# Four selective-scan layers on one NeuronCore: in the middle layers, one of the four input products of a scan group is made by TensorE

## The chip, the cores and the metric

The kernel runs on one NeuronCore of a Trainium2 chip, all in float32. The metric is the device time of one execution in microseconds. Six engines matter: PE (TensorE, with its weight loads apart as PEld), DVE (VectorE), ACT (ScalarE), POOL (GpSimd), SP (SyncE, which issues the DMAs) and the DMA engines themselves. SBUF is the memory that all of them read; PSUM takes what PE writes, in eight banks of 512 float32 per partition.

## The reference

The input is an image batch x of 4 x 48 x 48 x 192. Four layers follow each other, and all are built around the same selective scan. For channels d and 16 states n it is, in the words of the reference's second middle layer:

```python
def step(h_prev, t):
    x_t, dt_t, B_t, C_t = t
    dA = jnp.exp(dt_t[..., None] * A)
    dBx = (dt_t * x_t)[..., None] * B_t[:, :, None, :]
    h = dA * h_prev + dBx
    y = jnp.einsum('bkdn,bkn->bkd', h, C_t)
    return (h, y)
```

- Layer 0 is a bidirectional Mamba over the columns, a norm, and another over the rows: 16 passes over an image's 2304 tokens.
- Layers 1 and 2, the middle layers, are scans in four directions (rows, columns, both reversed) for each of four images: `dts, Bs, Cs` come from one projection of the input, `delta = softplus(dts @ W + bias)`, and the four results are summed. A norm, in layer 1 also a gate and a projection, closes each.
- Layer 3 runs short Mamba scans along each row and each column, and an MLP ends the network.

## The kernel before

**Tiling.** A pass over an image is cut into six jobs of 384 tokens (`CH`); a job's last states enter the next. In the middle layers the 192 channels are cut into three blocks of 64, and the 128 partitions hold a block twice: the upper half works on states 0 to 7, the lower on 8 to 15 (`parts` = 2). The eight states of each half make two groups of four (`NG`). A job so has 3 blocks x 2 groups = 6 steps, which I number as slots 0 to 5; the odd ones have group 1. Two layers, four images, four passes and six jobs make 192 jobs, 1152 steps. In layer 0 and in the rows (`parts` = 1) a block has 128 channels, a job four groups and 12 steps.

**One step**, for block i and group g:

- `decay` (L437), ACT: four `a = exp(delta * A)`, one per state. In the iteration before a new block, `enter` (L470) stands between the third and the fourth: the copy of `du` (delta times x) into a PSUM bank.
- `scan` (L475), DVE: the product `inputs = du * B` for all four states, 128 x 1540 (each state has 384 tokens and one entry column for the carried state), and one scan over the 1540 into `h`. `gather` puts its waits on an instruction ahead of it.
- `weigh` (L501), POOL: the last column of h is kept as the carried `state`, then h is multiplied by C in place. `carry` (L455) has written the states of the job before into B's entry column.
- `reduce` (L516), PE: four matmuls add the four states into `y` in PSUM, a half of the partitions each. With group 0, `skip` (L561) opens y: it adds the result of an earlier pass (`prior`) and, in the last pass of an image, the skip term D * x.

After the second group of a block, `take` copies y to `yc` (ACT), `gate` adds its two halves by a matmul into a `ps` buffer, and `close` (L577) copies that into a tile `o` (ACT), which is stored after the third block.

**The job ahead.** While a job runs, the next one's inputs are made (`units` L557, `projections` L383): in slot 1 the x_proj matmuls into a `ps` buffer and their copy `bcd`, which `spread` (L412) sends to memory as rows of B and C; in slot 2 the three `delta` (a matmul and an ACT softplus each). The softplus and the exp need different tables, so two table loads fall into each job. `fetch` (L422) brings B and C of one group back, each row spread over 64 partitions, two DMAs per group. `drive` (L465, POOL) multiplies delta by x for a block, into `dus`. Norm steps of the images before (`Side`) run in some slots on PE, ACT and POOL.

**What sets the order.** `run_jobs` (L1029) writes the order of every queue out by hand. Everything on ACT, POOL, DVE and PE runs in program order on its engine: L59 and L104 are the helpers through which the instructions pass, so most of them bear one of these two lines in the profile. In the middle layers, iteration t issues: scan(t), decay(t+2) with the fetch and the enter in it, close and take of an earlier block, carry(t+1), weigh(t), the next job's units, side work, gate (even t), drive (odd t), reduce(t-1). PSUM has one bank for y (L269), two rotating `ps` buffers (L270) for everything that PE makes on the side, four banks for `inputs` and one for `du`.

**What layer 0 and the rows have already.** There the class `MambaJob` overrides four of these functions. Two of the four products of a step are made by PE (`MADE` = 2): `turn` (L685) transposes du through a `ps` buffer, and ACT copies it to `duT`; `fill` (L710) multiplies duT by diagonal matrices with B's values on the diagonal, so that the product lands in a PSUM tile `made`. The diagonals come from memory: `spread` (L641) writes B's values, one element at a time, along the diagonals of zeroed buffers `dg`, and `fetch` (L662) brings them with the rows. DVE then multiplies only two states (`given`), and scans `made` by itself. There reduce runs two iterations behind the scan, not one.

The functions that the change touches, and what calls them:

Of the kernel before, what the change touches and what calls it, by code (L numbers as in the profile page):

```python
# [28 lines left out]
MADE = 2  # L29
LINE = 3 * MADE * 128  # L30

# [30 lines left out]
class K:  # L62
# [100 lines left out]
    def mean_weights(self, n):  # L163
        w = self.tile(self.const, [Q, Q], f"mean{n}")
        self.nc.vector.memset(w, 1.0 / n)
        return w
# [82 lines left out]
class ScanPools:  # L249
# [6 lines left out]
    def __init__(self, k, ctx, parts, rows):  # L256
# [6 lines left out]
        self.made = parts == 1  # L263
# [9 lines left out]
        self.given = NG - MADE if self.made else NG  # L273
# [7 lines left out]
        if self.made:  # L281
            self.made_inputs = k.tile(self.vec, [128, 1024], "made")[:, 512 - CH : 512 + CH]
            self.n_jobs = 0
            self.diags = []
            zeros = self.decays[2].rearrange("p j l -> p (j l)")[:, : LINE + 1]
            k.g.memset(zeros, 0.0)
            for n in range(2 * self.groups):
                d = k.dram([128 * (LINE + 1)], "dg")
                k.nc.sync.dma_start(d.rearrange("(t x) -> t x", x=LINE + 1), zeros)
                self.diags.append(d)  # L290
# [41 lines left out]
class ScanJob:  # L332
# [16 lines left out]
    def turn(self, i):  # L349
        pass  # L350

    def turn_back(self, i):
        pass

    def fill(self, i, g):
        pass
# [55 lines left out]
    def spread(self):  # L412

        self.bc = self.k.dram([2 * N, self.pools.W], "bc")
        self.k.nc.sync.dma_start(self.bc, self.bcd[: 2 * N, :])
# [6 lines left out]
    def fetch(self, g):  # L422

        k, pools = self.k, self.pools
        wide = pools.wide
        both = k.tile(pools.bcs, [128, 2, NG, pools.W], "bcb")
        self.bcb[g] = both[:, 0, :, :], both[:, 1, :, self.tokens]
        self.fetched[g] = []
        for m in range(pools.parts):
            at = (m * pools.groups + g) * 2 * NG  # L430
            ins = k.nc.sync.dma_start(
                both[m * wide : (m + 1) * wide].rearrange("p s j l -> p (s j l)"),
                self.bc[at : at + 2 * NG, :].rearrange("r l -> (r l)").partition_broadcast(wide),
            )
            self.fetched[g].append(ins)

    def decay(self, i, g, between=None):  # L437

        k, w, pools = self.k, self.w, self.pools
        if i == 0:  # L440
            self.fetch(g)
# [32 lines left out]

    def scan(self, i, g):  # L475

        k, pools = self.k, self.pools
        b, du, W = pools.b, pools.du, pools.W
        waits = self.waits.pop((i, g))
        if g == 0:  # L480
            waits.append(pools.entered)
        if pools.n_h >= pools.hbufs:
            of = pools.n_h - pools.hbufs
            waits += [pools.readers[of], pools.weighed[of]]
        pools.n_h += 1
        k.gather(waits)
        k.v.tensor_tensor(
            b, du.unsqueeze(1).to_broadcast([128, NG, W]), self.bcb[g][0], ALU.mult
        )
        step = -1 if self.rev else 1  # L490
        h = self.h[i, g] = k.tile(pools.hs, [128, NG, W], "h")
        k.v.tensor_tensor_scan(
            h.rearrange("p j l -> p (j l)")[:, ::step],
            self.a.pop((i, g)).rearrange("p j l -> p (j l)")[:, ::step],
            b.rearrange("p j l -> p (j l)")[:, ::step],
            0.0,
            ALU.mult,
            ALU.add,
        )
# [36 lines left out]
class DirJob(ScanJob):  # L536
# [11 lines left out]
    def load(self):  # L548
        k, two = self.k, self.pools.two
        self.xs = k.tile(two, [128, 3, CH], "xs")  # L550
        for m in range(2):
            k.nc.sync.dma_start(self.xs[m * 64 : (m + 1) * 64], self.part(self.src))
        if self.prior is not None:
            self.added = k.tile(two, [64, 3, CH], "added")
# [22 lines left out]
    def close(self, i):  # L577
        if i == 0:
            self.o = self.k.tile(self.pools.two, [64, 3, CH], "o")
        self.k.copy(self.o[:, i, :], self.ys)  # L580
        if i == 2:
            self.k.nc.sync.dma_start(self.part(self.dst), self.o)
# [5 lines left out]
class MambaJob(ScanJob):  # L588
# [52 lines left out]
    def spread(self):  # L641

        k, pools = self.k, self.pools
        sync = k.nc.sync
        n = pools.groups * (pools.given + NG)
        self.bc = k.dram([n, pools.W], "bc")
        sync.dma_start(self.bc, self.bcd[:n, :])
        be = k.dram([pools.groups, MADE, CH], "be")
        sync.dma_start(be.rearrange("g e l -> (g e) l"), self.bcd[n : 2 * N, self.tokens])
        at = pools.n_jobs % 2 * pools.groups  # L650
        pools.n_jobs += 1
        self.lines = pools.diags[at : at + pools.groups]
        for g in range(pools.groups):
            line = self.lines[g].rearrange("(t x) -> t x", x=LINE + 1)[:, :LINE]
            line = line.rearrange("t (b e c) -> t b e c", b=3, c=128)
            for e in range(MADE):
                with k.nc.allow_non_contiguous_dma(reason="diagonal"):
                    sync.dma_start(
                        line[:, :, e, 0:1], be[g, e].rearrange("(b t v) -> t b v", t=128, v=1)
                    )  # L660

    def fetch(self, g):  # L662

        k, pools = self.k, self.pools
        rows = pools.given + NG
        n = rows * pools.W
        t = k.tile(pools.bcs, [128, n + LINE], "bcb")
        both = t[:, :n].rearrange("p (j l) -> p j l", l=pools.W)
        self.bcb[g] = (
            both[:, : pools.given, :],  # L670
            both[:, pools.given :, self.tokens],
            t[:, n:].rearrange("p (b e c) -> p b e c", b=3, c=128),
        )
        ins = k.nc.sync.dma_start(
            t[:, :n],
            self.bc[g * rows : (g + 1) * rows, :]
            .rearrange("r l -> (r l)")
            .partition_broadcast(128),
        )
        k.nc.sync.dma_start(  # L680
            t[:, n:], self.lines[g][: 128 * LINE].rearrange("(t x) -> t x", t=128)
        )
        self.fetched[g] = [ins]

    def turn(self, i):  # L685

        k, pools = self.k, self.pools
        ps = k.tile(pools.ps, [128, 512], "ps")[:, :CH]
        self.turned_over(ps, self.du[i])
        self.duT[i] = k.tile(pools.two, [128, CH], "duT")  # L690
        k.copy(self.duT[i], ps)
        self.xd = k.tile(pools.one, [128, CH], "xd")
        k.act(self.xd, self.xs[:, i, :], AF.Identity, scale=self.w.D[:, i, :])
# [15 lines left out]

    def fill(self, i, g):  # L710

        k, pools = self.k, self.pools
        for b in range(3):
            at = slice(b * 128, (b + 1) * 128)
            for e in range(MADE):
                k.t.matmul(
                    pools.made_inputs[:, e * CH : (e + 1) * CH][:, at],
                    self.duT[i][:, at],
                    self.bcb[g][2][:, b, e, :],
                    start=True,  # L720
                    stop=True,
                    skip_group_check=True,
                )

    def scan(self, i, g):

        k, pools = self.k, self.pools
        waits = self.waits.pop((i, g))
        if g == 0:
            waits.append(pools.entered)  # L730
        if pools.n_h >= pools.hbufs:
            of = pools.n_h - pools.hbufs
            waits += [pools.readers[of], pools.weighed[of]]
        pools.n_h += 1
        k.gather(waits)
        n = pools.given
        du = pools.du.unsqueeze(1).to_broadcast([128, n, pools.W])
        k.v.tensor_tensor(pools.b, du, self.bcb[g][0], ALU.mult)
        step = -1 if self.rev else 1
        h = self.h[i, g] = k.tile(pools.hs, [128, NG, pools.W], "h")  # L740
        a = self.a.pop((i, g))

        def scan(at, tokens, b, first=0.0):
            k.v.tensor_tensor_scan(
                *(v[:, at, tokens].rearrange("p j l -> p (j l)")[:, ::step] for v in (h, a)),
                b[:, ::step],
                first,
                ALU.mult,
                ALU.add,
            )  # L750

        scan(slice(0, n), slice(0, pools.W), pools.b.rearrange("p j l -> p (j l)"))
        if pools.rows:
            scan(slice(n, NG), self.tokens, pools.made_inputs)
            return
        for e in range(MADE):
            at = g * NG + n + e
            first = 0.0 if self.prev is None else self.prev.state[:, i, at : at + 1]
            scan(
                slice(n + e, n + e + 1),  # L760
                self.tokens,
                pools.made_inputs[:, e * CH : (e + 1) * CH],
# [1393 lines left out]
```

## Time and profile before

| | us |
|---|---|
| median of 3 runs (18010.82 to 18017.85) | 18016.21 |
| the profiled execution | 18024.41 |
| its span, from the first instruction to the last | 18022.6 |
| layer 0 | about 49 to 5700 |
| inputs of the middle layers (convolutions, norm) | about 5700 to 6080 |
| middle layers | about 6080 to 12145 |
| rows | about 12300 to 17600 |
| MLP | to the end |

Busy over the whole span, from the page: PE 16243.2 us (90%), DVE 16418.0 (91%), ACT 13776.3 (76%), POOL 14149.0 (79%). A share of the whole is a mean over stages that differ, so the stages are read one by one. A group line names source line, engine, operation, output and inputs by the program's names, then count, busy time and mean duration in ns, then how long the engine stood idle ahead of it and what ended that. In a timeline each line has start and duration in us, and in brackets the idle time before it. PE records two matmul passes for each float32 matmul, one for a transpose, and its durations contain the pipeline's drain, so starts are the better measure of its pace.

### The profile page before, as it was taken

The numbers are of one execution on the slowest core, as the hardware profiler recorded it, in microseconds if no ns is written. First come the engines' busy times: TensorE is split into PE (matmuls) and PEld (weight loads), VectorE is DVE, ScalarE is ACT, GpSimd is POOL, SyncE is SP. The second block draws the span as 40 slices with busy tenths as digits, with TensorE's granted clock in tenths as the row PEclk, the third lists the DMA queues.
The fourth block names the chain that finished last, engine by engine and source line by source line (L and its number), as shares of the span: only waits on it lengthen the run. The fifth ranks groups of instructions, "written<-read, shape, count | busy, mean of one in ns | idle before, by whom it ended". The sixth has DMA issues, their size and how long they took to land. (4 is left out here: it accounts for less than half of the span.)

```text
span 18022.6 us, 313028 instructions
## 1 busy us (share of the span) xinstructions
PE 16243.2 (90%) x118512; PEld 10759.8 (60%) x118512; DVE 16418.0 (91%) x10747; ACT 13776.3 (76%) x25601; POOL 14149.0 (79%) x10862
## 2 busy tenths in 40 slices
PE   9999999999999777787777877878999999999999
PEld 7787787888885322222222222226888888888874
DVE  8899899999996799999999999996999999999992
ACT  7888888888885567777777777777888888888874
POOL 7877878878874488888888888876888888888880
PEclk9999999999999878788888887789999999999999
DMA  4343343333333466666666666663343343433431
GB/s 137 122 128 124 125 134 122 128 126 128 128 126 93 105 137 146 151 148 153 152 148 149 144 150 140 147 145 112 122 127 125 120 124 123 132 123 122 125 118 50
DMA packets 1229187, 2324.58 MB, mean 129 GB/s; under 512 B 704376, under 2 KB 962016, under 8 KB 1075232
## 3 DMA queue, kind: packets, MB, share of 16 engines
q1 hardware_dynamic: 1227680, 2304.55, 46.8%
q8 instruction: 938, 15.37, 0.4%
q14 instruction: 569, 4.66, 0.1%
HBM read 2105.57 MB, written 200.98 MB: 128 GB/s over the span
## 5 line engine op out<-in xcount | busy, mean ns | idle before, releaser
L59 POOL TENSOR_TENSOR h<-h,bcb 128x1536 f32<-128x1536 f32 x3456 | 11312.2, 3273 | 798.6 <-DVE h L59 499.1
L104 ACT ACTIVATE a<-delta,A 128x384 f32<-128x384 f32 (+1 forms) x13824 | 7377.6, 603 | 911.7 <-DVE h L59 901.2
L59 DVE TENSOR_TENSOR_SCAN h<-a,inputs 128x770 f32<-128x770 f32 (+2 forms) x3456 | 7915.9, 2290 | 146.5 <-DVE inputs L59 1.8
L59 DVE TENSOR_TENSOR inputs<-du,bcb 128x770 f32<-128x770 f32 (+2 forms) x3456 | 4256.4, 1232 | 287.2 <-POOL bcb L59 100.9
L59 PE MATMUL made<-bcb,duT 128*128 128x128 f32 x27648 | 3559.6, 279 | 172.1 <-DVE h L59 139.6
L59 PEld LDWEIGHTS y<-ident,h 128*128 128x128 f32 x27648 | 3119.8, 142 | 845.0 <-issue 485.7
L59 PE MATMUL y<-ident,h 128*128 128x128 f32 x27648 | 3508.5, 277 | 59.8 <-ACT yt L104 49.2
L59 PEld LDWEIGHTS made<-bcb,duT 128*128 128x128 f32 x27648 | 3341.4, 195 | 273.9 <-DVE h L59 178.7
L59 PE MATMUL y<-h,sum 128*64 128x384 f32 x9216 | 2661.7, 643 | 750.2 <-POOL h L59 547.4
L59 DVE TENSOR_TENSOR_SCAN h<-a,made 128x768 f32<-128x768 f32 (+1 forms) x1536 | 2343.2, 1536 | 263.2 <-PE made L59 256.4
L59 PEld LDWEIGHTS y<-h,sum 128*64 128x64 f32 x9216 | 848.7, 167 | 2175.9 <-issue 982.2
L59 DVE TENSOR_TENSOR_SCAN h<-a,state,made 128x384 f32<-128x384 f32 x1920 | 1827.8, 993 | 221.1 <-PE made L59 219.4
L59 POOL COPY state<-h 128x4 f32<-128x4 f32 x2304 | 434.4, 189 | 1908.5 <-DVE h L59 1879.5
L59 PE MATMUL ps<-bcd,dtT 12*128 12x384 f32 (+1 forms) x2304 | 1076.9, 580 | 245.1 <-ACT delta L104 240.2
L59 PE MATMUL ps<-u,inT 96*128 96x384 f32 x3456 | 1251.7, 489 | 38.8 <-DMA u<-xn_wh 27.1
L104 ACT ACTIVATE delta<-ps,vec 128x384 f32<-128x384 f32 x1152 | 636.4, 577 | 344.3 <-PE ps L59 338.2
L59 PEld LDWEIGHTS ps<-bcd,dtT 12*128 12x128 f32 (+1 forms) x2304 | 415.1, 206 | 808.8 <-ACT delta L104 487.3
L59 PE MATMUL ps<-yt,outT 128*96 128x384 f32 x2304 | 808.7, 488 | 0.4 <-POOL yt L59 0.4
L59 PE MATMUL ps<-xh,diag 32*32 32x192 f32 x32256 | 796.8, 324 | 4.0 <-ACT xc L104 2.3
L59 PEld LDWEIGHTS ps<-u,inT 96*128 96x128 f32 x3456 | 600.5, 191 | 304.0 <-issue 36.4
L104 ACT ACT_TABLE_LOAD x603 | 773.6, 1283 | 10.6
L101 ACT ACT_TABLE_LOAD x600 | 769.8, 1283 | 9.8 <-PEq L2146 0.7
(147 smaller groups left out, 15082.7 us busy)
## 6 DMA issues: line engine op xcount, KB each, us to landing
bcb<-bc SPq DMA_DIRECT2D x768, 770.0 KB
bcb<-bc SPq DMA_DIRECT2D x384, 1155.0 KB
bcb<-bc SPq DMA_DIRECT2D x384, 1152.0 KB
bcb<-dg SPq DMA_DIRECT2D x768, 384.0 KB
y<-o SPq DMA_DIRECT2D x192, 288.0 KB
xs<-xi_wh SPq DMA_DIRECT2D x96, 288.0 KB
xs<-xi_hw SPq DMA_DIRECT2D x96, 288.0 KB
added<-y SPq DMA_DIRECT2D x96, 288.0 KB
```

Source lines behind the costliest of these rows:

```text
L59: return lambda *a, **kw: self.tc.keep_in_program_order(op(*a, **kw))
L101: self.in_order(self.nc.scalar.preload_act_table_set(LOG_EXP))
L104: return self.in_order(self.nc.scalar.activation(out, in_, func, **kw))
```

## The change

`MADE` becomes a table: two made products with `parts` = 1, one with `parts` = 2. The functions `spread`, `fetch`, `turn`, `fill` and `scan` of `MambaJob` move into the base class, written for both cases, so that the middle layers use them as well. A middle step then has three products on DVE (128 x 1155), a scan over these, and a scan of 384 over the made one, which starts from the carried state. `fill` makes the fourth product with two matmuls per 128 tokens, one for each half of the partitions. PSUM: three banks for `inputs`, one for `made`.

In `run_jobs` the fetch leaves `decay` and gets a place of its own after the scan, four groups ahead in the middle layers (two, as before, elsewhere). `turn` stands at the end of an even iteration, behind reduce and ahead of fill; `drive` goes from three groups ahead to four. `close` writes into the tile `added`, which held the prior's part, now with three buffers and taken in every pass; `o` goes. The weights of the 96-channel mean move from a lasting pool into that of their stage. On the host, the rows of the x_proj weights are put in the new order.

```diff
-MADE = 2
-LINE = 3 * MADE * 128
+MADE = {1: 2, 2: 1}
...
-        self.made = parts == 1
+        self.made = MADE[parts]
+        self.turned = parts == 1
+        self.line = 3 * self.made * parts * 128
...
-        self.given = NG - MADE if self.made else NG
+        self.given = NG - self.made
...
     def spread(self):
-        self.bc = self.k.dram([2 * N, self.pools.W], "bc")
-        self.k.nc.sync.dma_start(self.bc, self.bcd[: 2 * N, :])
+        k, pools = self.k, self.pools
+        sync, parts, made = k.nc.sync, pools.parts, pools.made
+        n = parts * pools.groups * (pools.given + NG)
+        self.bc = k.dram([n, pools.W], "bc")
+        sync.dma_start(self.bc, self.bcd[:n, :])
+        be = k.dram([parts, pools.groups, made, CH], "be")
+        sync.dma_start(be.rearrange("m g e l -> (m g e) l"), self.bcd[n : 2 * N, self.tokens])
...
+            for e in range(made):
+                for m in range(parts):
+                    with k.nc.allow_non_contiguous_dma(reason="diagonal"):
+                        sync.dma_start(
+                            line[:, :, e, m, 0:1],
+                            be[m, g, e].rearrange("(b t v) -> t b v", t=128, v=1),
+                        )
...
     def decay(self, i, g, between=None):
         k, w, pools = self.k, self.w, self.pools
-        if i == 0:
-            self.fetch(g)
...
+    def turn(self, i):
+        k, pools = self.k, self.pools
+        wide = pools.wide
+        ps = k.tile(pools.ps, [128, 512], "ps")[:, : 3 * wide]
+        for b in range(3):
+            k.t.matmul(
+                ps[:, b * wide : (b + 1) * wide],
+                self.du[i][:wide, b * 128 : (b + 1) * 128],
+                k.ident[:wide, :wide],
...
+        self.duT[i] = k.tile(pools.two, [128, 3, wide], "duT")
+        k.copy(self.duT[i].rearrange("p b d -> p (b d)"), ps)
+
+    def fill(self, i, g):
+        k, pools = self.k, self.pools
+        wide = pools.wide
+        for b in range(3):
+            for e in range(pools.made):
+                at = e * CH + b * 128
+                for m in range(pools.parts):
+                    k.t.matmul(
+                        pools.made_inputs[m * wide : (m + 1) * wide, at : at + 128],
+                        self.duT[i][:, b, :],
+                        self.bcb[g][2][:, b, e, m, :],
...
     def scan(self, i, g):
...
+        scan(slice(0, n), slice(0, pools.W), pools.b.rearrange("p j l -> p (j l)"))
...
+        for e in range(pools.made):
+            at = g * NG + n + e
+            first = 0.0 if self.prev is None else self.prev.state[:, i, at : at + 1]
+            scan(
+                slice(n + e, n + e + 1),
+                self.tokens,
+                pools.made_inputs[:, e * CH : (e + 1) * CH],
+                first,
+            )
...
     def close(self, i):
-        if i == 0:
-            self.o = self.k.tile(self.pools.two, [64, 3, CH], "o")
-        self.k.copy(self.o[:, i, :], self.ys)
+        self.k.copy(self.added[:, i, :], self.ys)
         if i == 2:
-            self.k.nc.sync.dma_start(self.part(self.dst), self.o)
+            self.k.nc.sync.dma_start(self.part(self.dst), self.added)
...
-    behind = 2 if jobs[0].pools.made else 1
-    ahead, taken, gated, driven = 2, behind + 1, behind + 2, 2 + behind
+    behind = 2 if jobs[0].pools.turned else 1
+    ahead, taken, gated, driven = 2, behind + 1, behind + 2, 4
+    fetched = 2 * ahead if behind == 1 else ahead
...
+        if t + fetched < len(groups) and groups[t + fetched][1] == 0:
+            job, i, g = groups[t + fetched]
+            job.fetch(g)
...
-        if soon := at_group(t + 2, 0):
+        if behind == 2 and (soon := at_group(t + 2, 0)):
             soon[0].turn(soon[1])
...
         if 0 <= t - behind < len(groups) and behind == 1:
             job, i, g = groups[t - behind]
             job.reduce(i, g)
+        if behind == 1 and (soon := at_group(t + 2, 0)):
+            soon[0].turn(soon[1])
         if t + 1 < len(groups):
             job, i, g = groups[t + 1]
             job.fill(i, g)
```

## The prediction, made before the change was run

> **What bounds the kernel now.** I read the windows by stage first, then the groups of instructions inside the middle stage and inside layer 0 (which already has what the change brings), then the timeline of one job. By stage (columns: busy time of PE, weight load, DVE, ACT, POOL, then granted clock, DMA share, GB/s):
>
> ```profile
> 6080.00:12145.00 6065.00, 4714.70 (x14810) 1607.45 (x14810) 5910.93 (x2304) 4404.79 (x8203) 5032.24 (x4284) 0.80 0.65 146
> 49.00:5700.00 5651.00, 5562.26 (x48933) 4497.28 (x48933) 5182.31 (x4641) 4651.70 (x8699) 4445.95 (x4197) 0.98 0.39 125
> 12300.00:17600.00 5300.00, 5084.91 (x51911) 4228.68 (x51909) 4982.67 (x3457) 4290.40 (x8000) 4607.83 (x2322) 0.99 0.40 124
> ```
>
> The first line is the stage that changes: DVE is busy 5911 of 6065 us (97%), and PE runs at a mean clock of 0.80. The other two stages keep their instructions. [...] The groups from 7000 to 11000 us:
>
> ```profile
> L59 POOL TENSOR_TENSOR h<-h,bcb 128x1536 f32<-128x1536 f32 x761 | 2621.2, 3444 | 61.5 <-POOL state L59 0.7
> L59 DVE TENSOR_TENSOR_SCAN h<-a,inputs 128x1540 f32<-128x1540 f32 x761 | 2557.7, 3361 | 29.3 <-DVE inputs L59 0.5
> L59 DVE TENSOR_TENSOR inputs<-du,bcb 128x1540 f32<-128x1540 f32 x761 | 1347.0, 1770 | 66.7 <-POOL bcb L59 22.6 <-PE y L59 10.0 <-ACT du L104 7.5
> ```
>
> 761 steps in 4000 us are 5.26 us each, 31.5 per job. DVE sets the pace and waits for almost nothing. The same groups in layer 0, 1000 to 5000 us:
>
> ```profile
> L59 POOL TENSOR_TENSOR h<-h,bcb 128x1536 f32<-128x1536 f32 x828 | 2410.8, 2912 | 66.8 <-POOL state L59 0.6
> L59 DVE TENSOR_TENSOR_SCAN h<-a,inputs 128x770 f32<-128x770 f32 x827 | 1453.0, 1757 | 30.1
> L59 DVE TENSOR_TENSOR_SCAN h<-a,state,made 128x384 f32<-128x384 f32 x1367 | 1301.4, 993 | 158.3 <-PE made L59 157.0
> L59 DVE TENSOR_TENSOR inputs<-du,bcb 128x770 f32<-128x770 f32 x828 | 797.1, 963 | 53.0 <-POOL bcb L59 52.3 <-DMA bcb<-bc 0.4
> ```
>
> Last, the timeline of one middle job, ACT from slot 1 to slot 3, with PE's x_proj matmuls and the DVE product that ends the stretch:
>
> ```profile
> 9016.65 2.14 PE L59 MATMUL ps<-xs,xpT 64*44 64x384 f32 x6
> 9018.13 0.47 ACT L104 ACTIVATE o<-ps 64x384 f32<-64x384 f32 x1
> 9018.87 0.48 ACT L104 ACTIVATE bcd<-ps 44x384 f32<-44x384 f32 x1
> 9020.51 2.13 ACT L104 ACTIVATE a<-delta,A 128x384 f32<-128x384 f32 x4 [1.16 <-DVE h L59]
> 9022.66 1.28 ACT L104 ACT_TABLE_LOAD   x1
> 9023.96 1.05 ACT L104 ACTIVATE delta<-ps,vec 128x384 f32<-128x384 f32 x2
> 9026.27 0.58 ACT L104 ACTIVATE delta<-ps,vec 128x384 f32<-128x384 f32 x1 [1.26 <-PE ps L59]
> 9026.87 1.28 ACT L101 ACT_TABLE_LOAD   x1
> 9028.17 1.63 ACT L104 ACTIVATE a<-delta,A 128x384 f32<-128x384 f32 x3
> 9029.70 0.47 ACT L104 ACTIVATE du<-dus 128x384 f32<-128x384 f32 x1
> ...
> 9030.91 1.77 DVE L59 TENSOR_TENSOR inputs<-du,bcb 128x1540 f32<-128x1540 f32 x1
> ```
>
> Slots 1 to 3 are where ACT is nearly late: with bcd, three deltas and two table loads in its queue it has du ready at 9030.17, and DVE wants it at 9030.91. The margin is 0.74 us, once per job.
>
> **The change, part by part.** *DVE, the gain.* Between the 770 and 1540 rows, a product of 1155 is 1.37 us and its scan 2.56; the single made scan is 0.99. From start to start (layer 0: product 0.99, scan 1.68, made scan 0.91; the middle product of 1540 1.81) a step is 1.40 + 2.48 + 0.91 = 4.79 against 5.20 now. That is 0.41 x 1152 = 472 us, if nothing else is late: 28.7 us per job.
>
> *PE, what is added.* Per step `fill` adds six matmuls of 128 columns, two passes each. Layer 0's passes start 0.11 apart. These write half the columns each, and the reduce's half-width matmuls run in pairs (eight passes in 1.3 us at full clock), so I take 0.75 (between 0.67 paired and 1.33 unpaired). `turn` adds three transposes every second step, 0.35, and an ACT copy of 128x192, 0.35 to 0.4 (192 columns take 0.42 and 384 take 0.48 in layer 0). This work alone would fit: PE's queue has room at 0.80 clock. What matters is where it stands.
>
> *ACT now waits for PE.* The copy to duT closes the even iteration in ACT's order, behind nothing but the transposes; those stand on PE behind the gate and the reduce of the step before. Until they have run, everything behind the copy waits: the next four decays, du, o, yc and, in slot 1, bcd. Those in turn hold PE: the next block's y has one PSUM buffer, so its skip and reduce wait for yc, and `fill` stands behind that reduce. This is a loop from duT copy to duT copy, each link behind the other. At full clock: decays, du, o, yc 3.35; skip 0.5 (0.65 or 1.3 in the passes with a prior, 0 in the others; a lone matmul is 0.65); reduce 1.3; fill 0.75; gate 0.65; reduce 1.3; turn 0.35, drain 0.2, copy 0.35; hand-overs 0.15. Sum 8.9 us for two steps, in which DVE needs 9.58. It fits with 0.7 to spare.
>
> *In slots 1 to 4 it doesn't fit.* `turn` also takes one of the two `ps` buffers. So slot 1's x_proj finds the gate's buffer still unread until the o copy, where today it takes the other one and starts early (9016.65, before o). From the end of the duT copy of slot 0: o ends at 3.0; x_proj, six passes, 1.95 plus drain 0.2; bcd ends at 5.73; four decays 7.85; table load 9.15; three deltas 11.3 (the third waits for its matmul: at full clock 1.58 us from first to third, the least in the trace); on PE, the gate, reduce and turn behind the third delta's matmul end at 12.75; duT copy 13.3. That pair takes 13.3 us, not 8.9. The next (slots 3 and 4) begins with the second table load: 10.6. The last takes 9.3. Sum **33.2 us per job**, against 31.5 now and 28.7 for DVE. On DVE it shows as waits for du in slot 4 (some 2 us) and for `made` in slots 2 to 4. Price: (33.2 - 31.5) x 192 = +326 us.
>
> *The clock.* The loop leaves PE idle before the skips (2.5 to 5 us, each ended by yc) and busy in between. The trace: in this stage the clock is 0.80, and the reduce's pairs start 0.64 apart instead of 0.325 when it is halved; layer 0, with PE full, has 0.98. The Trainium skill, "TensorE: Matmul & The Clock Gate", Part 1, says that half rate follows an idle window of some 3.4 us and full rate a busy one. By the rule, the two idle stretches over 3.4 us in a job cost 1.7 us of PE time each, +3.4 per job or 650 us, against the change. By the row, more work for PE should lift the mean clock above 0.80 (bound below: 0). Part of the loss falls where DVE has slack; I take +1.0 us per job, +190 us, as the row says that short idle stretches stay at full clock.
>
> *POOL.* One weigh is 3.44 us here, 2.91 in layer 0, 3.46 in the rows. C starts 6160, 3080 and 3072 bytes into its tile; the Trainium skill, "SBUF — State Buffer", Specifications, has 16-byte lines, and only layer 0's C starts within one. After the change it starts at 4620, within one too; I take 2.91 (ends 2.91 and 3.44). Either way POOL does two weighs, four small copies and a dus in 7.9 to 8.9 us, and the loop leaves it more, so it costs nothing here; at 28.7 us per job the slow value would be late where a normalisation step falls beside dus.
>
> *DMA.* B and C shrink from 3.15 to 2.76 MB per job, the diagonals add 0.79 MB; share 0.65 stays near that. On SP, four diagonal writes (0.53 to 0.63 us each in layer 0) stand ahead of the first fetch, so it starts about 0.8 later than now, but the second no longer waits behind the y store. Both are needed some 18 to 24 us later. Cost 0 in a 33 us job; up to 0.5 us per job (100 us) if DVE ran at its best.
>
> *The rest.* Four zero fills at the stage's start: some 5 us. Outputs in the prior's tile and the moved mean96: 0, no instruction more. dus one slot earlier: behind a weigh, needed four steps on: 0. Layer 0 and the rows: 0, the same queues.
>
> Sum against the profiled execution (18024.4, span 18022.6): 326 + 190 + 5 = +521, so 18545; the median of the runs lies 8 us lower: **about 18535**.
>
> **Rivals.** *Faster:* ACT and PE hide all this, because hand-overs overlap more than I count, and DVE stays the bound at 29.5 us per job: 2.0 x 192 = -384, **17632**. For it: in 0.80 clock PE still has a fifth of its time idle, and layer 0 lives with such copies. Against: layer 0 has twelve steps for the same table loads and reduces two steps behind; here the margin of du is 0.74 us and I add 3.8 to its chain while DVE comes 0.8 earlier. *The clock decides:* with half clock in most reduces, 35.5 to 36.5 us per job: +770 to +960, **18790 to 18980**; for it speaks the 0.80 of today at similar idle stretches. *A draw:* half of the jobs have no skip, and for them the loop gives 31.7, today's pace; if the others are shortened alike: **18020**.
>
> **How the numbers follow.** My forecast (18250 to 18750) 0.50, the clock 0.26, faster 0.19, draw 0.05. Within 0.2% (36 us) is what a measurement can't tell from no change: 0.04; slower 0.77. The range reaches from part of the faster case, 17850, to the top of the clock's, 18980.
>
> **What would show it.** Right: DVE's busy share in the stage falls below 90%, with waits on ACT du and PE made; ACT waits on PE ps at the duT copy, about 1.6 us in slot 2; x_proj starts after the o copy. Wrong: DVE still over 95% busy and steps of 4.8 to 4.9 us; or waits on POOL bcb or DMA dg at its head. A fill of 1.3 instead of 0.75 would add 0.5 us per step to the loop and point to the clock's figure.

## The result, and the profile after

The changed kernel took **19063.76 us** (median of four runs, 19052.41 to 19069.51) against 18017.03 for the kernel before on the same chip: a ratio of 1.0581, interval 1.0562 to 1.0599. The forecast was 18535, with a range up to 18980. The direction and the place were right; the loss is twice what was forecast, 1047 us instead of 519.

The windows by stage, after (columns as before: busy time of PE, weight load, DVE, ACT, POOL, then clock, DMA share, GB/s):

```profile
6080.00:13180.00 7100.00, 5728.03 (x30302) 2724.82 (x30299) 5564.29 (x3451) 4479.08 (x8764) 5017.33 (x4279) 0.82 0.61 136
49.00:5700.00 5651.00, 5563.93 (x48958) 4494.01 (x48958) 5190.33 (x4645) 4652.57 (x8700) 4445.63 (x4197) 0.98 0.39 125
13340.00:18640.00 5300.00, 5085.31 (x51916) 4226.63 (x51914) 4982.38 (x3457) 4292.04 (x8003) 4605.83 (x2322) 1.00 0.39 124
```

The whole loss lies in the middle stage, which grew from 6065 to 7100 us. DVE was busy for 97% of it and is busy for 78% now, although it has less to do. Layer 0 and the rows are as they were. DVE got what the forecast gave it, as the groups from 7000 to 12000 us show; what is new stands behind the bar, in the idle time:

```profile
L58 POOL TENSOR_TENSOR h<-h,bcb 128x1536 f32<-128x1536 f32 x809 | 2792.0, 3451 | 65.5 <-PE ps L58 0.2
L58 DVE TENSOR_TENSOR_SCAN h<-a,inputs 128x1155 f32<-128x1155 f32 x809 | 2070.6, 2559 | 30.5
L58 DVE TENSOR_TENSOR inputs<-du,bcb 128x1155 f32<-128x1155 f32 x808 | 1103.9, 1366 | 351.9 <-ACT du L103 247.8 <-POOL bcb L58 78.6 <-DMA bcb<-bc 4.9
L58 DVE TENSOR_TENSOR_SCAN h<-a,state,made 128x384 f32<-128x384 f32 x676 | 677.9, 1003 | 585.4 <-PE made L58 583.8
```

The product takes 1.37 us and its scan 2.56, to the digit what was taken between the neighbouring rows; the made scan 1.00. The waits over the same 5000 us (some 135 jobs; total, times, longest) say who is late:

```profile
ACT duT L103 <- PE ps L58: 1143.3, 404, 7.9
DVE h L58 <- PE made L58: 699.4, 417, 4.4
PEld y L58 <- ACT yc L103: 538.6, 206, 4.5
DVE inputs L58 <- ACT du L103: 247.8, 165, 2.3
```

ACT stands 1143 us at the duT copy, PE stands at y until ACT has copied yc, and DVE waits for both of their products: the loop that the prediction describes, read off the trace. To see where in a job it hurts, I counted the steps of the stage from its first product (start of a product to start of the next, mean over the jobs, us):

```
kernel              slot 0     1     2     3     4     5     job   waits for made / for the next product of 0.3 us or more
before                5.36  5.21  5.21  5.30  5.20  5.25   31.54   -
after                 5.52  5.33  5.28  8.39  7.17  5.36   37.05   made 0.6 in 0, 0.4 in 2, 1.6 in 3, 2.3 in 4; product 0.4 after 1 and 5, 1.8 after 3
e1_turn_first         5.34  5.13  5.07  6.47  5.11  5.17   32.30   made 1.4 in 3; product 0.4 after 0, 0.3 after 5
e5_warm_two           5.44  5.43  5.19  7.96  5.70  5.31   35.04   made 0.5 in 0, 0.3 in 2, 1.3 in 3, 0.8 in 4; product 0.4 after 1 and 5, 1.7 after 3
e6_behind_two         4.86  5.31  5.15  9.61  4.78  5.22   34.92   made 0.3 in 2, 4.7 in 3; product 0.3 after 1 and 5
e10_all_third         5.14  5.25  5.18  8.22  4.83  6.05   34.67   made 0.3 in 0, 0.4 in 2, 2.3 in 3, 0.8 in 5; product 1.0 after 3, 0.4 after 5
e11_turn_third        5.06  4.97  4.88  5.94  9.85  4.97   35.67   made 0.4 in 3, 5.0 in 4; product 0.6 after 3
e13_two_late          5.82  5.52  5.20  5.51  4.79  5.86   32.70   made 0.9 in 0, 0.4 in 1, 0.3 in 2, 0.6 in 5; product 0.6 after 3, 0.3 after 5
e17_turn_zero         5.12  4.94  4.92  6.38  5.19  4.96   31.50   made 1.4 in 3, 0.3 in 4
e18_fill_ahead        5.27  4.96  4.95  5.43  5.49  4.95   31.06   made 0.6 in 4; product 0.5 after 3
```

Slots 3 and 4 carry 6.0 of the 8.3 us by which a job exceeds DVE's own 28.7. This stretch of the timeline is slot 3 and the start of slot 4, from the late duT copy on (lines left out are marked):

```profile
9031.23 0.33 ACT L103 ACTIVATE duT<-ps 128x192 f32<-128x192 f32 x1 [3.52 <-PE ps L58]
9031.58 1.28 ACT L100 ACT_TABLE_LOAD   x1
...
9032.87 1.63 ACT L103 ACTIVATE a<-delta,A 128x384 f32<-128x384 f32 x3
...
9034.40 0.47 ACT L103 ACTIVATE du<-dus 128x384 f32<-128x384 f32 x1
...
9035.01 1.37 DVE L58 TENSOR_TENSOR inputs<-du,bcb 128x1155 f32<-128x1155 f32 x1 [1.95 <-ACT du L103]
...
9035.69 0.47 ACT L103 ACTIVATE yc<-y 128x384 f32<-128x384 f32 x1
...
9036.26 2.83 PE L58 MATMUL y<-h,sum 128*64 128x384 f32 x8 [4.26 <-issue]
...
9038.85 1.52 PE L58 MATMUL made<-bcb,duT 128*64 128x128 f32 x12
```

ACT waits 3.5 us for the transposes; table, decays and du follow, and DVE gets du 1.95 us late. yc is last. Only then does PE begin its reduce, after 4.26 us of idleness, and it runs at half clock: 2.83 us for eight passes, and 1.52 for the fill behind them. DVE's next made scan waits for that fill. The same two pieces of work at full clock, earlier in this trace:

```profile
9013.90 1.51 PE L58 MATMUL y<-h,sum 128*64 128x384 f32 x8 [0.78 <-ACT yc L103]
...
9015.21 0.85 PE L58 MATMUL made<-bcb,duT 128*64 128x128 f32 x12
```

### The profile page after: what moved, and what is told of

The parts are those of the page before. It is cut to its first block, busy times and chain, and to the rows that moved or that the text cites. A ratio compares the mean times of both kernels' runs of the same rounds, so it can differ in the third digit from the quotient of the medians.

```text
span 19063.2 us, 346188 instructions
## 1 busy us (share of the span) xinstructions
PE 17259.6 (91%) x134064; PEld 11873.0 (62%) x134064; DVE 16081.6 (84%) x11899; ACT 13857.6 (73%) x26177; POOL 14141.4 (74%) x10863
## 3 DMA queue, kind: packets, MB, share of 16 engines
q14 instruction: 587, 4.81, 0.1%
## 5 line engine op out<-in xcount | busy, mean ns | idle before, releaser
L58 DVE TENSOR_TENSOR_SCAN h<-a,inputs 128x770 f32<-128x770 f32 (+2 forms) x3456 | 6993.2, 2024 | 146.1 <-DVE inputs L58 1.4
L58 PE MATMUL made<-bcb,duT 128*128 128x128 f32 (+1 forms) x41472 | 4726.9, 290 | 189.3 <-DVE h L58 142.6
L58 PEld LDWEIGHTS made<-bcb,duT 128*128 128x128 f32 (+1 forms) x41472 | 4316.3, 183 | 667.9 <-issue 348.0
L58 DVE TENSOR_TENSOR inputs<-du,bcb 128x770 f32<-128x770 f32 (+2 forms) x3456 | 3791.6, 1097 | 680.1 <-ACT du L103 378.5
L58 DVE TENSOR_TENSOR_SCAN h<-a,state,made 128x384 f32<-128x384 f32 x2880 | 2790.7, 997 | 1035.3 <-PE made L58 1031.9
L58 PE MATMUL y<-h,sum 128*64 128x384 f32 x9216 | 2765.7, 641 | 682.1 <-issue 380.3
L58 DVE TENSOR_TENSOR_SCAN h<-a,made 128x768 f32<-128x768 f32 (+1 forms) x1728 | 2525.1, 1471 | 441.9 <-PE made L58 434.0
L103 ACT ACTIVATE duT<-ps 128x384 f32<-128x384 f32 (+1 forms) x1152 | 470.8, 409 | 2132.4 <-PE ps L58 2130.7
L58 PE MATMUL ps<-bcd,dtT 12*128 12x384 f32 (+1 forms) x2304 | 973.4, 530 | 98.7 <-ACT delta L103 93.4
L58 PE MATMUL y<-added,ident 64*64 64x384 f32 x576 | 328.1, 658 | 633.0 <-ACT yc L103 632.3
```

Of the source, the lines that this page charges most:

```text
L58: return lambda *a, **kw: self.tc.keep_in_program_order(op(*a, **kw))
L103: return self.in_order(self.nc.scalar.activation(out, in_, func, **kw))
```

## The experiments

Two theories stood after this reading. **Order:** the loss comes from where turn and fill stand in PE's queue. **Clock:** the loop would be nearly harmless if PE didn't fall to half rate in it. A third was the prediction's own claim about the ps buffers. Each experiment changes the middle layers alone.

**1. turn ahead of the next job's projections and deltas.** Its input, dus, is ready much earlier.

```diff
+        if behind == 1 and (soon := at_group(t + 2, 0)):
+            soon[0].turn(soon[1])
         stream.run(at if at < per - 1 else per)
...
-        if behind == 1 and (soon := at_group(t + 2, 0)):
-            soon[0].turn(soon[1])
```

> The changed kernel with one edit: in the middle layers turn (three transposes and the copy to duT) stands ahead of the stream of units, so ahead of side work, gate and reduce, and takes its ps buffer there. Theory (the loop duT copy -> decays, o, yc -> skip, reduce -> fill -> gate, reduce -> turn -> duT copy sets the pace): the duT copy no longer waits for a reduce, x_proj no longer waits for the o copy, and the waits for du and made nearly go; a middle job falls from 37.1 us to 29.5 to 31, the time to about 17500 to 17900. Rival 1 (PE with its added work at a clock of 0.82 is simply the bound, in whatever order): the job stays above 35 us, the time above 18650. Rival 2 (B, C and diagonals come too late): waits of DVE for POOL bcb or of PE for dg take over, time 18000 to 18500.

18185.29 us, ratio 1.0095 (1.0079 to 1.0112): 878 of the 1047 us come back from one move. The waits over the same window as above:

```profile
ACT duT L103 <- PE ps L58: 541.0, 405, 5.3
DVE h L58 <- PE made L58: 335.6, 177, 5.7
DVE inputs L58 <- POOL bcb L58: 146.8, 137, 4.0
```

Both of the large waits are halved, DVE's for du is gone, and PE's granted clock in the stage rises from 0.82 to 0.90, since PE no longer stands so long. It still missed its range, which ended at 17900: 1.4 us of waiting for made stay in slot 3.

**2. The ps buffer.** turn's PSUM tile is taken ahead of gate, so that x_proj can't be the one that has to wait for the o copy (in the changed kernel `added<-ps`).

```diff
+        if behind == 1 and (soon := at_group(t + 2, 0)):
+            soon[0].turn_ps = soon[0].k.tile(soon[0].pools.ps, [128, 512], "ps")
         if done := at_group(t - gated, last_group):
             done[0].gate(done[1])
```

> The changed kernel with one edit: turn takes its ps buffer ahead of the gate, and issues its transposes where it did. So the x_proj of slot 1 gets the buffer that the duT copy frees, not the one that the o copy frees. Theory (the second ps wait is worth its place in the loop): x_proj starts some 2.5 us earlier in a job, the stretch from the duT copy of slot 0 to that of slot 2 falls from 13.2 to 10.7 to 11.5 us, the time by 300 to 480 us to 18580 to 18760; waits of ACT duT on PE ps remain. If the buffer doesn't matter: within 80 us of 19064.

19058.76 us: no effect. In the changed kernel itself x_proj starts before that copy, in the job shown and in 190 of 191 jobs of its trace:

```profile
9019.03 2.12 PE L58 MATMUL ps<-xs,xpT 64*38 64x384 f32 x6
...
9020.99 0.47 ACT L103 ACTIVATE added<-ps 64x384 f32<-64x384 f32 x1
```

The prediction's claim is refuted.

**3 and 5. Keeping PE's clock up.** Six matmuls of 192 columns that nobody reads follow the fill of an iteration with a turn (e3), or only of those for slots 2 and 4 (e5), to shorten the idle stretch. They cost PE time themselves, so each gain is a lower bound.

```diff
             job.fill(i, g)
+        if behind == 1 and at and (soon := at_group(t + 2, 0)):
+            soon[0].warm(soon[1])
```

(e3 has the same lines without `and at`.)

> The changed kernel with six added matmuls of 192 columns after each fill that follows a turn, into the turn's own ps tile once it has been copied; nobody reads them. They cost PE 1.95 us at full clock, 3.9 at half, in a stretch in which it otherwise waits for yc. Theory (the missing 3 to 4 us per job are PE at half clock, which idle stretches bring on): the middle stage's clock rises from 0.82 to 0.9 or more, a job falls from 37.1 to 33.5 to 35.5 us, the time to 18370 to 18760. If half clock is not what was mis-sized, added work on PE in the loop can only cost: 19064 or more.

> As e3_warm, but the six unread matmuls follow only the turns of slots 2 and 4, ahead of PE's two longest idle stretches; the stretch from slot 0 to slot 2, which had no room for them, is left as in the changed kernel. Theory (half clock is the mis-sized term, and e3 paid for its warmth in that stretch): duT copy to duT copy from slot 0 to 2 stays at 13.2 us or less, the other two stretches fall from 13.4 and 10.4 to below 12 and 10; a job 34.5 to 35.8 us, the time 18560 to 18820, most of it in the jobs with both skips. If the clock is worth no more than the 0.7 us per job of e3: 18900 to 19000.

e3 took 18924.01 us (1.0502): the stage's clock rose from 0.82 to 0.94, but it missed its range. From the duT copy of slot 0 to that of slot 2, where PE has no long idle stretch, the added matmuls were in the way: that pair of steps grew from 13.3 to 14.1 us, while the next one fell from 13.3 to 11.7. e5 met its own range and took 18705.40 (1.0383, interval 1.0362 to 1.0404): 358 us less than the changed kernel, by work that computes nothing. The reduce of slot 2, which ran at half rate in all 192 jobs of the changed kernel, does so in 50 of e5's. PE at half clock cost at least 1.9 us per job (358 us over 192 jobs; in the two profiles 37.05 and 35.04).

**4. The weigh.** h begins four bytes later, so that the addresses of h and C differ by 8 modulo 16 and not by 12.

> The changed kernel with the tile h of the middle layers begun one element (4 bytes) later, so that h and C stand 8 bytes apart within 16, as they do in layer 0. Theory (the distance of the two operands within 16 bytes sets the weigh's duration): the middle weigh falls from 3.45 us to 2.91. Rival: it stays at 3.45 and layer 0's 2.91 has another cause. In both cases the time stays within 150 us of 19064, since POOL is not in the loop but for the wait for it in the odd reduces.

19063.12 us, the same time. But the instruction changed, in the groups of e4:

```profile
L58 POOL TENSOR_TENSOR h<-h,bcb 128x1536 f32<-128x1536 f32 x807 | 2345.5, 2906 | 65.3 <-POOL state L58 0.2
```

2.91 us instead of 3.45. The time is of a single run. POOL was not on the path, as the prediction said; the reason that it gave for the duration was wrong.

**6, 7, 8. More room for PE, and earlier rows.** e6 reduces two iterations behind, as layer 0 does (`behind = 2`), with the fetch still four ahead; e7 is e1 with the rows of both groups fetched ahead of the diagonals; e8 joins e6, that fetch and the shift of h.

> The changed kernel with reduce two iterations behind the scan in the middle layers too, as in layer 0: take and enter come ahead of the decays on ACT, reduce(t-2) and turn follow the stream, ahead of side work and gate. It removes both links of the loop: the duT copy waits for no weigh of the running step, and the yc copy for no decays. Theory: a middle job falls to 29.5 to 31.5 us, the time to 17500 to 17950, below the kernel before; what is left are waits for B and C (POOL bcb, DMA dg) of 1 us per job. Rival (PE's work in program order, not the links, sets the pace): no better than e1_turn_first, 18100 to 18300.

> e1_turn_first with the fetch taken apart: the rows of both groups are requested first, the two diagonals behind them, so the second group's rows no longer stand on SP behind the wait for the diagonal writes. In e1 DVE waited 0.9 us per job for the carry into bcb, and PE 0.4 for dg. Theory (late B and C cost what these waits show): 0.6 to 1.2 us per job, 115 to 230 us, 17950 to 18070. If other waits take their place: within 60 us of 18185.

> e6_behind_two with the fetch of e7 and the h tile of e4 (weigh 2.91 us). Theory: with the loop cut, rows early and POOL lighter, DVE sets the pace again at 28.9 to 30 us per job; the time 17450 to 17650, DVE over 95% busy in the stage. If the clock or PE still binds: no better than e6.

18660.25 (1.0359), 18227.70 (1.0118) and 18606.21 us (1.0329): all three missed. In e7 DVE's waits for rows fell, but PE's for the diagonals rose from 69 to 207 us. In e6 and e8 five of the six slots are good, 4.8 to 5.3 us, and slot 3 alone loses 4.7 to 4.8 us for `made`: turn is again behind the deltas there, and so is fill(3).

**9, 10, 11. The third delta behind fill(3).** Its matmul waits for the softplus of the first, which stands in ACT behind a table load. The same edit is made on e6, e8 and (with h shifted, and du's copy first in slot 3) on e1.

```diff
+        third = per == 6 and at == 2 and len(stream.units) == 4
+        if third:
+            stream.units, held = stream.units[:3], stream.units
         stream.run(at if at < per - 1 else per)
...
             job.fill(i, g)
+        if third:
+            stream.units = held
+            stream.run(at)
```

> Kernel e6_behind_two (reduce two iterations behind in the middle layers), and of the next job's three deltas in slot 2 the third goes behind fill(3) on PE. In e6 the steps from slot 1 on last 5.33, 5.16, 9.62, 4.78, 5.23 and 4.85 us, and the 9.62 has 4.73 us of DVE waiting for made: fill(3) stands on PE behind a delta matmul that waits for ACT. Theory (what is left is this one place in PE's order): that step falls to about 4.9, the job from 35.0 to 30.3 us, 192 x 4.7 = 900 us less: 17750, between 17650 and 17900. Rival (PE at half clock or POOL is late anyway, and the wait comes back a slot later): above 18300. Second rival (the third delta, later now, makes du late in slot 4): a DVE wait for ACT du of 2 us or more there, 18000 to 18200.

> Kernel e8_two_split_shift with the same move of the third delta behind fill(3). In e8 the steps from slot 1 on last 5.08, 5.09, 9.76, 4.78, 5.01 and 4.90, with 4.87 us of waiting for made in the 9.76. Theory: 29.8 us per job instead of 34.6, 920 us less than e8: 17690, between 17600 and 17850. Rival (the wait comes back elsewhere): above 18300. If e9 meets its figure and this one does too, the difference of the two (some 60 us) is what the earlier rows of B and C and the shorter weigh are worth.

> Kernel e1_turn_first (turn ahead of the stream, reduce one behind), with h four bytes later, the third delta behind fill(3), and in slot 3 the copy of du ahead of the decays instead of behind the third. In e1 the steps from slot 1 on last 5.13, 5.05, 6.44 (1.40 of it waiting for made), 5.09, 6.01 (1.15 of it waiting for the next product's input) and 5.28. Theory: both waits go, 30.4 us per job instead of 33.0, 490 us less than e1: 17700, between 17600 and 17900. Rival (one behind, the skip that waits for yc and the reduce at half clock still hold fill up): 18050 to 18250.

18642.99 (1.0354), 18586.75 (1.0317) and 18809.36 us (1.0444): the theory that one place was all that was left fell. In e9 and e10 half of slot 3's wait stays, and du of slot 4 and `made` of slot 5 are late instead. e10's timeline, slot 2 to 3, shows what holds PE now:

```profile
8985.44 0.47 ACT L103 ACTIVATE added<-ps 64x384 f32<-64x384 f32 x1
...
8985.96 1.64 PE L58 MATMUL ps<-bcd,dtT 6*128 6x384 f32 x2 [1.48 <-ACT added L103]
...
8987.53 1.54 PE L58 MATMUL y<-added,ident 64*64 64x384 f32 x2
...
8989.00 2.83 PE L58 MATMUL y<-h,sum 128*64 128x384 f32 x8
...
8992.27 1.03 PE L58 MATMUL made<-bcb,duT 128*64 128x128 f32 x12
8992.38 0.33 ACT L103 ACTIVATE duT<-ps 128x192 f32<-128x192 f32 x1 [4.10 <-PE ps L58]
...
8993.35 0.95 DVE L58 TENSOR_TENSOR_SCAN h<-a,made 128x384 f32<-128x384 f32 x1 [4.81 <-PE made L58]
```

The second delta's matmul waits for a ps buffer until ACT's close copy, which stands behind four decays; then skip, reduce and fill follow at half clock, and DVE has waited 4.81 us. So a ps buffer does matter, but for a delta and in this order. In e11, where delta 3 is late, ACT's du, table, decays and yc are late behind it, and slot 4 pays 5.0 us.

**12, 13, 14. What stands ahead of fill.** e12 is e10 with close ahead of the decays; e13 is e8 with the second and third delta behind fill(3) (`units[:2]` in the diff above); e14 is e1 with h shifted and take and close ahead of the decays. (In e12's expectation the list of e10's steps begins at slot 2, not at slot 1; the table above counts from the stage's first product. The expectations of e11 and e14 give 6.01 us for e1's slot 5, that of e18 gives 5.78 for e17's; over all jobs of their traces it is 5.17 and 4.96, so the wait of 1.15 us that e11 set out to remove was not there.)

> Kernel e10_all_third with close (ACT's copy added<-ps, which frees the buffer for the second delta's matmul) ahead of the four decays in the middle layers. In e10 the steps from slot 1 on last 5.12, 8.24, 4.83, 6.09, 5.14 and 5.27 us. Theory (the hand-over of the ps buffer is the rest): 8.24 falls to 5.2 and 6.09 to 5.5, the job from 34.7 to 31.1, 690 us less: 17900, between 17750 and 18100. Rival (PE's half clock in skip, reduce and fill is the rest, whatever they wait for): over 18400.

> Kernel e8_two_split_shift with the second and the third delta of slot 2 behind fill(3) on PE, so that nothing of PE's queue ahead of fill(3) waits for ACT's close or softplus but the first delta, whose buffer is free. Theory (fill is late because of what waits ahead of it): made is ready in slots 2 and 3; du of slot 4 is late by 0 to 1.5 us, as its ACT queue has two deltas after fill; job 30.5 to 31.5, 17850 to 18050. Rival (half clock): over 18300.

> Kernel e1_turn_first with h four bytes later and with take and close (yc, added<-ps) ahead of the four decays on ACT in the middle layers: skip and reduce, and fill behind them, no longer wait for the decays. In e1 the steps from slot 1 on last 5.13, 5.05, 6.44, 5.09, 6.01 and 5.28. Theory (yc behind the decays is the rest of the loop): 6.44 falls to 5.2 and 6.01 to 5.2, the job from 33.0 to 30.9, 400 us less than e1: 17780, between 17650 and 17950. Rival (half clock, or the third delta's place): 18080 to 18200.

18245.38 (1.0124), 18218.43 (1.0108) and 18336.56 us (1.0178). The first two take 341 and 388 us off their bases. Slot 3 falls from 8.22 to 5.87 us in e12 and from 9.72 in e8 to 5.51 in e13, so what waits ahead of fill(3) is the larger part of that slot's loss; but slot 0 in e12, and slots 0 and 5 in e13, give 0.5 and 1.8 us back, and neither run reaches its figure. e14 is slower than e1: ACT, in order, now stands for y of PE (768 us of 5000), and du of slot 4 is 2.2 us late. A copy moved forward in a queue pays where its input is ready: e12's close waits for PE nowhere in the 5000 us. Where it isn't, as for yc in e14, the wait falls on everything behind.

**15, 16, 17. A transfer that begins late.** e13's timeline, ACT, POOL and SP:

```profile
8541.93 0.48 ACT L103 ACTIVATE bcd<-ps 38x384 f32<-38x384 f32 x1
...
8546.24 0.09 POOL L58 MEMSET bcd<- 38x1 f32 x1
...
8546.36 0.33 SPq L414 DMA_DIRECT2D bc<-bcd  x1
```

bcd is complete at 8542.4 but for one column, whose zero fill is queued on POOL behind a weigh; the write to memory waits 4 us for it. Over all jobs of e13 it begins 2.4 us after bcd on the mean (4.1 in e1). In the three runs the tile is opened and that column zeroed when the job is loaded: on e13, on e13 with close first, and on e1 with h shifted.

```diff
         self.added = k.tile(two, [64, 3, CH], "added", 3)
+        self.open_bcd()
```

> Kernel e13_two_late, and in the middle layers POOL's zero fill of bcd's entry column stands at the start of the job, ahead of a weigh, not behind it. In e13 bcd was ready at 8542.4 and its write to memory began at 8546.4, behind that fill. Theory: B's rows and the diagonals come 4 us earlier, PE's wait for the diagonals (268 us of 5000, 1.8 us per job) and DVE's for rows go: 30.8 us per job instead of 32.8, 390 us less: 17830, between 17700 and 17980. Rival (the transfers themselves are slow, or the half clock holds fill up all the same): 18150 to 18230.

> Kernel e15_zero_early with close ahead of the decays, as in e12. Theory: the second delta no longer waits for close, du of slot 4 is 0.6 us earlier in most jobs: 50 to 120 us below e15. Rival (deltas stand behind fill anyway): within 40 us of e15.

> Kernel e1_turn_first with h four bytes later and the zero fill of bcd at the start of the job. e1's waits for transfers are 1.0 us per job, and POOL's weigh falls by 0.54 us. Theory: 1.0 to 1.5 us per job less: 17900 to 18000. Rival: within 60 us of e1 (18130 to 18240).

18128.85 (1.0063), 18099.99 (1.0045) and **17991.66** us (0.9984, interval 0.9977 to 0.9991). e15 gained 90 of the 390 us expected: its write begins 0.5 us after bcd, 1.9 earlier than in e13 and not 4, and PE's wait for the diagonals fell only from 268 to 188 us. e16 lies 29 us below e15, inside its rival's bound. e17 gained 194 us on e1 and met its figure: its waits for POOL's rows fell from 147 to 67 us. It makes two edits at once, and how the 194 us divide between them was not measured. The shorter weigh has a part: the median step of slots 1 and 5 falls from 4.98 or 4.99 to 4.79 us in e17, and from 5.00 to 4.79 in e4, which has the shift alone.

**18. fill(3) ahead of gate and reduce(1)**, which it doesn't need, on e17.

```diff
+        if per == 6 and at == 2 and t + 1 < len(groups):
+            job, i, g = groups[t + 1]
+            job.fill(i, g)
         if done := at_group(t - gated, last_group):
             done[0].gate(done[1])
```

> Kernel e17_turn_zero, and in slot 2 fill(3) stands ahead of gate and reduce(1) on PE, behind the third delta. In e17 the steps from slot 1 on last 4.92, 4.89, 6.32 (1.40 of it waiting for made), 5.15, 5.78 and 5.06. Theory (gate and reduce in front of fill are the rest): 6.32 falls to 5.0 or 5.1, 1.2 us per job or 230 us less than e17: 17760, between 17700 and 17880. Rival (the third delta waits for ACT, and the reduce that comes later makes yc and the next fill late): 17950 to 18050.

**17929.91** us, ratio 0.9951 (0.9938 to 0.9965): 62 us less than e17, not 230. Its waits, in the same window:

```profile
ACT duT L103 <- PE ps L58: 478.9, 359, 5.3
DVE h L58 <- PE made L58: 178.0, 146, 4.2
DVE inputs L58 <- POOL bcb L58: 92.5, 138, 4.2
DVE inputs L58 <- ACT du L103: 70.1, 62, 2.1
```

DVE's wait for made is a quarter of the changed kernel's. The range ended at 17880, so it missed it. Slot 3 gained 0.95 us, slot 4 gave 0.3 back, as the later reduce makes the next y late. This version beats both kernels: 0.5% under the kernel before, 6% under the changed one.

## Why the prediction was right in part and wrong in part

- **DVE's gain: right.** 1.37 and 2.56 us as interpolated. In e6 and e8 an undisturbed step takes 4.78, the forecast's 4.79. The gain was there and could not be collected.
- **The loop through the duT copy: right as a mechanism.** A late duT copy, then du in slot 4 (forecast 2 us, measured 1.8), made in slots 3 and 4; e1, which only moves turn, brings back 878 us. The three pairs of steps, from duT copy to duT copy, were forecast at full clock as 13.3, 10.6 and 9.3 us and lasted 13.3, 13.3 and 10.4.
- **x_proj behind the o copy: wrong.** e2 shows no effect, and x_proj starts before that copy. The first pair took its 13.3 us for another reason. In the 96 jobs without a skip it lasts 11.2 us where the reduce behind the third delta runs at full rate (35 jobs) and 12.9 where it runs at half (59); over all jobs it is 11.3 us where both reduces of the pair run at full rate. The forecast put some 2 us too much on x_proj and, at full clock, nothing on half rate: the sum agreed by accident.
- **The clock term: mis-sized, and this is the step that failed.** I read the row as "short idle stretches stay at full clock" and took +1.0 us per job, 190 us, against +3.4 and 650 us by the rule of the Trainium skill ("TensorE: Matmul & The Clock Gate", Part 1). e5 gives at least 1.9 us per job. In the second pair, forecast 10.6 and measured 13.3, one reduce (2.83 - 1.51) and one fill (1.52 - 0.85) at half rate are 2.0; in the first pair it takes some 1.7 to 2 more, by the comparison of jobs above. The mean of 0.80 before could not say what a slow reduce costs: the reduce behind the third delta ran at half rate in 171 of 192 jobs there too, and DVE, always busy, hid it.
- **The rule behind that term: supported, but not the whole.** I counted the reduces that open right after idle time of PE in the changed kernel's middle stage (half rate: passes of 0.85 us, full rate: 0.49). Of 96 after more than 3.5 us all ran at half rate, of 122 after 0.3 to 2 us one did, and of the 59 between them 21. With the rule the forecast would have been 326 + 650 + 5 = 981 above, or 18997, against +1047 measured. But that nearness is partly luck: the prediction counted two stretches over 3.4 us per job, and the trace has one (193 in 192 jobs). Half rate also came without a long stretch. The reduce behind the third delta ran at half rate in 135 of 192 jobs, with at most 1.0 us of idle time at a stretch in the 8 us before it:

```profile
9024.08 1.55 PE L58 MATMUL ps<-bcd,dtT 6*128 6x384 f32 x4
...
9026.18 0.91 PE L58 MATMUL ps<-bcd,dtT 6*128 6x384 f32 x2 [0.55 <-ACT delta L103]
...
9027.61 3.25 PE L58 MATMUL y<-h,sum 128*64 128x384 f32 x7
```

Why PE falls to half rate there is open. It still does so in e17 (133 of 192 jobs), and e18, which takes fill(3) out from behind this reduce, gains 0.95 us in slot 3.

- **The fill's 0.75: right** (0.85 to 0.88 with the drain at full clock). **The weigh: wrong**, 3.45 us and not 2.91; its price of 0 was right (e4). **DMA cost 0: right** in the changed kernel (5 us of DVE's waits in 5000); it becomes a wait only where the rest is faster, as in e7 and e13.
- **Rivals.** "The clock decides", at 18790 to 18980, was nearest, and still too low. That order and clock make each other worse (a late yc makes PE idle, idleness halves its rate, and the slow reduce makes fill, turn and the next yc late) fits the timeline of slots 3 and 4, but no run measures it apart.

How the 1047 us divide between order and clock can't be said by subtraction, since e1 removes both: the reordered queue also keeps PE busier (0.90), and the reduce of slot 2 runs at half rate in 43 jobs and no longer in 192. That the clock alone costs at least 358 us is shown by e5. For order alone there is no figure; that e1 is 520 us faster than e5 at a lower mean clock (0.90 against 0.93) speaks for it, though e5's time contains its added matmuls. Still open is what the 2.3 us per job between e18 (31.06) and DVE's own 28.7 are in detail. Its trace shows waits for made, du and rows; no run took all of them away together.

## What to carry to other kernels

When work is moved to an engine with time to spare, list what stands ahead of it in that engine's program order and what each of those waits for: here one move of three transposes past matmuls that wait for ACT was worth 878 us, more than the change could ever gain. Where an in-order loop leaves PE idle for more than some 3.5 us, cost the work behind that stretch at half rate, even if the stage's mean clock looks harmless; and read the pace of each group of matmuls in the trace, since here one ran at half rate in 135 of 192 jobs without such a stretch. And move a copy forward in its engine's order only where its input is ready by then: close moved ahead of the decays gained 341 us (e12), yc moved ahead with it cost 151 against e1 (e14).

## What the runs showed of the hardware

The duration of POOL's 128x1536 multiplication in place followed the distance of its two operands' addresses modulo 16 bytes, with only h moved between the changed kernel and e4: 3.45 us at a distance of 12, 2.91 at 8. The addresses are counted as offsets in their tiles; where the tiles themselves begin is not shown. The prediction's reading, that C's place within a 16-byte line decides, is not it: C stood at the same offset in both.

PE ran at half rate after every idle stretch of more than 3.5 us that a reduce of the changed kernel opened from (96 of 96). It also ran so, without such a stretch, behind the third delta (135 of 192); why is open.
